# Mish of the last edge group and the last node chunk: from a rational form on VectorE to Exp, Ln and Tanh on ScalarE

## The chip, the cores and the metric

The kernel runs on one core of one Trainium2 chip. A core has five engines that run side by side, each with its own instruction queue in a fixed order: TensorE (PE in the profile; its weight loads are PEld), VectorE (DVE), ScalarE (ACT), GpSimd (POOL) and SyncE (SP). The metric is the time of one execution in microseconds (us). The median of three runs before the change is 1883.51 us (1879.14 to 1885.42).

## The reference

A network of four layers over a graph of 625 nodes with 512 features and 20000 edges. Each layer normalizes the nodes' features, applies a ReLU, computes messages along the edges, sums them by target node, and adds the result to the features. The change touches only the last of the four layers:

```python
def mish(x):
    return x * jnp.tanh(jax.nn.softplus(x))

# N = 625 nodes, E = 20000 edges (sorted by dst), 512 features, 64 edge features
edge_feat = jnp.concatenate([x[src], x[dst], edge_attr], axis=-1)
h = mish(edge_feat @ W1 + b1)
messages = mish(h @ W2 + b2)
agg = jax.ops.segment_sum(messages, dst, num_segments=x.shape[0])
u = mish(jnp.concatenate([x, agg], axis=-1) @ W3 + b3)
out = u @ W4 + b4
y = x + out
mu = jnp.mean(y, axis=-1, keepdims=True)
var = jnp.mean(jnp.square(y - mu), axis=-1, keepdims=True)
return (y - mu) * jax.lax.rsqrt(var + LN_EPS) * gamma + beta
```

Mish of v is v times tanh(ln(1 + exp(v))). With e = exp(v) and n = (2 + e) * e the factor tanh(ln(1 + e)) is also n / (n + 2), which needs an exponential and a reciprocal only.

## The kernel before

**Tiles and stages.** The 20000 edges are 160 tiles of 125 edges, taken in groups of G = 4, so there are NG = 40 groups, numbered 0 to 39. The 625 nodes are NC = 5 chunks of 125, numbered 0 to 4. All arithmetic is fp32.

`layer3_near` (from L1116) is the last layer. Its loop over steps s (L1349) is a pipeline written out by hand: in step s the first product of group s is computed (`first`), the second product of group s - 2 (`second`, L1235), and the messages of group s - 4 are summed into their target nodes (`sent`, L1251) and, one step later, added to the table `aT` of sums (`collected`, L1274). Instructions wrapped in `keep` stay in program order on their engine, so each engine's order is the order of these calls.

**Mish in the steady state.** A result is first bounded from above on VectorE (`bounded`, L1180, into a tile `uz`, `um` or `uu`), then `quotients` (L1188) puts Exp on ScalarE, then Ln with a bias of 1, then Tanh, for all tiles that are ready in that step; a product on VectorE ends it. ScalarE computes functions from a loaded set of tables; where the next function isn't in the set, a load of another set (ACT_TABLE_LOAD) stands ahead of it. Exp and Tanh stand in one set here, Ln in another, so each round has two loads.

**The last group.** Group 39 is treated apart. `second` bounds its messages `mess` in two halves of two tiles each (L1246 to L1248), 125x1024 elements, into two `uz` tiles. In the step of its second product (L1383 to L1388) ScalarE computes Exp of both halves, then Ln and Tanh of half 0 alone. In `sent` (L1255 to L1258) VectorE makes half 1's mish by the rational form, `times_quotient` (L1197), and then half 0's by one product. After that TensorE sums the group's messages by a product with the one-hot matrix `oh` (L1267, tile `agg`); VectorE copies that out (L1271, `ag`), TensorE transposes it (L1277, `trs`) and VectorE adds it to `aT` (L1278).

**The last chunk.** When the last sums are in `aT`, `update_u(4)` (L1285) multiplies them with the lower half of W3 (L1288, tile `u`), adds the part of the nodes' own features (L1291), and bounds the result (L1183, tile `uu`). ScalarE computes Exp (L1408), and then chunk 3's square root for its normalization (`update_root(3)`, L1328, with a load of its set). VectorE makes the chunk's mish by `times_quotient`. Then come the transposes (`update_turn`, L1302, copied out at L1304), chunk 3's end (`update_end(3)`, L1330: a reciprocal of the root, two operations, an output DMA), and chunk 4's product with W4 in two halves (`update_out`, L1319, tile `o`), its statistics, root and end.

Of the kernel before, what the change touches and what calls it, by code (L numbers as in the profile page):

```python
# [9 lines left out]
F32 = mybir.dt.float32  # L10
F16 = mybir.dt.float16
I32 = mybir.dt.int32
AF = mybir.ActivationFunctionType
ALU = mybir.AluOpType
# [3 lines left out]
D = 512  # L18
# [3 lines left out]
G = 4  # L22
NG = NT // G
# [120 lines left out]
def gnn_body(ctx: ExitStack, tc: tile.TileContext, a: dict, out: bass.AP, consts, near: bool):  # L144

    nc = tc.nc
# [969 lines left out]
    def layer3_near(wts, wm2, own, h_tabs, uh):  # L1116

        keep = tc.keep_in_program_order
        with tc.tile_pool(name="layer3n", bufs=2) as lp, banks("c", 6):
# [3 lines left out]
            edges, zs, ms, us, acc, nodes = {}, {}, {}, {}, {}, {}  # L1123
            W = 32

            def base_of(g):
                return min(max(math.ceil(g * G * PACE - SLACK), 0), N - W)
# [26 lines left out]
            def rows(g):  # L1154

                rt = lp.tile([128, GE], F32, tag="rt", name="rt", bufs=3)
                ge = slice(g * GE, (g + 1) * GE)
                nc.sync.dma_start(rt[:64, :], a["edge_attr_64"][:, ge])
                if g < NW:

                    base = min(max(math.floor(g * G * PACE) - 24, 0), N - 64)
                    keep(nc.sync.dma_start(wx[g][:64, :], a["L3_gnn_W1"][2 * D:, :]))
                    keep(nc.sync.dma_start(wx[g][64:, :], xd[base:base + 64, :]))
                    keep(nc.sync.dma_start(dn[g], bcast(a["dst_row"][0, ge], GE, 64)))
                    keep(nc.vector.tensor_scalar(rt[64:, :], dn[g], float(base), row[64:, :],
                                                 op0=ALU.subtract, op1=ALU.is_equal))
                else:
                    nc.sync.dma_start(rt[64:, :], a["edge_attr_64"][:, ge])
                gs = []
                for j in range(G):  # L1170
                    gs.append(lp.tile([P, D], F32, tag="gath", name="g_s", bufs=12))
                    keep(gather(xs, src_i, g * G + j, gs[-1]))
                edges[g] = rt, gs

            def rows_added(g):

                for j in range(G):
                    keep(gather(xd, dst_i, g * G + j, edges[g][1][j], compute_op=ALU.add))

            def bounded(v, parts, cols, tag, bufs):  # L1180

                u = lp.tile([128, width.get(tag, cols)], F32, tag=tag, name=tag, bufs=bufs)[:parts, :cols]
                keep(nc.vector.tensor_scalar_min(u, v, 20.0))  # L1183
                return u
# [3 lines left out]
            def quotients(v):  # L1188

                for u in v:  # L1190
                    keep(nc.scalar.activation(u, u, AF.Exp))  # L1191
                for u in v:
                    keep(nc.scalar.activation(u, u, AF.Ln, bias=1.0))
                for u in v:
                    keep(nc.scalar.activation(u, u, AF.Tanh))

            def times_quotient(v, e):  # L1197

                n = lp.tile([128, G * D], F32, tag="um", name="n", bufs=1)[:v.shape[0], :v.shape[1]]
                keep(nc.vector.scalar_tensor_tensor(n, e, 2.0, e, op0=ALU.add, op1=ALU.mult))  # L1200
                keep(nc.vector.tensor_scalar_add(e, n, 2.0))
                keep(nc.vector.reciprocal(e, e))
                keep(nc.vector.tensor_mul(n, n, v))
                keep(nc.vector.tensor_mul(v, n, e))

            def flat(v):
                return v.rearrange("p a b -> p (a b)")
# [43 lines left out]
            def sent(g):  # L1251


                m = ms.pop(g)
                if g == NG - 1:  # L1255
                    v = [flat(m[:, 2 * n:2 * n + 2, :]) for n in range(2)]
                    times_quotient(v[1], us.pop(("m", g, 1)))
                    keep(nc.vector.tensor_mul(v[0], v[0], us.pop(("m", g, 0))))  # L1258
                base = base_of(g)
                acc[g] = pools["acc"].tile([128, 128], F32, tag="acc", name="agg3", bufs=2)  # L1260
                o = work.tile([P, G, W], F32, tag="oh", name="oh")
                nc.vector.tensor_tensor(o, iota_f[:, None, base:base + W].to_broadcast([P, G, W]),
                                        dst_f[:, g * G:(g + 1) * G, None].to_broadcast([P, G, W]),
                                        op=ALU.is_equal)
                for j in range(G):
                    for i in range(KD):
                        nc.tensor.matmul(acc[g][i * W:(i + 1) * W, :], o[:, j, :],  # L1267
                                         m[:, j, i * 128:(i + 1) * 128], start=j == 0, stop=j == G - 1,
                                         skip_group_check=True, tile_position=(0, i * W))
                v = lp.tile([128, 128], F32, tag="ag", name="ag", bufs=2)  # L1270
                keep(nc.vector.tensor_copy(v, acc[g]))  # L1271
                acc[g] = v
# [22 lines left out]
            def update_mul(c):  # L1295
                keep(nc.vector.tensor_mul(nodes[c], nodes[c], us.pop(("u", c))))
# [52 lines left out]
            for s in range(NG + 5):  # L1349
                if s + 2 < NG:  # L1350
                    rows(s + 2)
                if NW <= s + 1 < NG:
                    rows_added(s + 1)
                if 6 <= s < 9:
                    later_weights(s - 6)
                if s < NG:
                    first(s)
                if s == 0:
                    for n in range(2):
                        quotients([us["z", 0, n]])  # L1360
                        z = flat(zs[0][:, n])
                        keep(nc.vector.tensor_mul(z, z, us.pop(("z", 0, n))))  # L1362
                if s - 4 in ms and s - 4 < NG - 1:
                    m = flat(ms[s - 4])
                    keep(nc.vector.tensor_mul(m, m, us.pop(("m", s - 4))))
                if s - 3 in ms and s - 3 < NG - 1:
                    us["m", s - 3] = bounded(flat(ms[s - 3]), P, G * D, "um", 1)
                quotients([us[k] for k in (("z", s, 0), ("m", s - 3), *(("u", c) for c in range(NC - 1) if s - 6 == last_of[c])) if k in us])
                for c in range(NC - 2):
                    if s - 9 == last_of[c]:  # L1370
                        update_root(c)
                if s - 1 in zs and s > 1:
                    z = flat(zs[s - 1][:, 0])
                    keep(nc.vector.tensor_mul(z, z, us.pop(("z", s - 1, 0))))
                for c in range(NC - 1):
                    if s - 7 == last_of[c]:
                        update_mul(c)
                if s == 1:
                    second(0)
                    keep(nc.vector.memset(mT, 0.0))  # L1380
                if 1 <= s - 2 < NG:
                    second(s - 2)
                if s - 2 == NG - 1:  # L1383

                    for n in range(2):
                        keep(nc.scalar.activation(us["m", NG - 1, n], us["m", NG - 1, n], AF.Exp))
                    for fn, b in ((AF.Ln, 1.0), (AF.Tanh, 0.0)):
                        keep(nc.scalar.activation(us["m", NG - 1, 0], us["m", NG - 1, 0], fn, bias=b))  # L1388
                for c in range(NC - 1):
                    if s - 7 == last_of[c]:  # L1390
                        update_turn(c)
                    if s - 8 == last_of[c]:
                        update_out(c)
                    if s - 9 == last_of[c] and c < NC - 2:
                        update_end(c)
                if 9 <= s < 9 + NC:
                    biases(s - 9)
                if 0 <= s - 4 < NG:
                    sent(s - 4)
                if 0 <= s - 5:  # L1400
                    collected(s - 5)
                for c in range(NC - 1):
                    if s - 5 == last_of[c]:
                        update_u(c)
            c = NC - 1
            update_u(c)
            e = us.pop(("u", c))
            keep(nc.scalar.activation(e, e, AF.Exp))  # L1408
            update_root(c - 1)
            times_quotient(nodes[c], e)  # L1410
            update_turn(c)
            update_end(c - 1)
            update_out(c)
# [19 lines left out]
    with tc.tile_pool(name="wts3", bufs=1) as wts:  # L1433
# [3 lines left out]
        if near:  # L1437
            keep = tc.keep_in_program_order
# [67 lines left out]
```

## Time and profile before

| | |
|---|---|
| median of 3 runs | 1883.51 us (1879.14 to 1885.42) |
| profiled execution | 1883.0 us |
| its span | 1881.2 us |
| mean granted TensorE clock | 0.983 |
| TensorE busy | 1772.1 us, 94% of the span |
| VectorE busy | 1074.1 us, 57% |
| ScalarE busy | 741.3 us, 39% |
| GpSimd busy | 809.9 us, 43% |
| chain that ended last | TensorE 83%, VectorE 11%, ScalarE 2%, DMA 2%, issue 1% |

The profile is of one execution, recorded by the chip's hardware profiler. Times in its rows count from the span's start. A group of equal operations is shown as line, engine, operation, output tile and inputs, shapes (partitions x elements) and count; `<-` in brackets names what ended the wait before it. "The chain that ended last" is followed back from the last instruction, at each step to what released it. Busy shares are averages over the whole span; a change in the last 50 us is read from those 50 us. The granted clock is what the throttle gave TensorE, as a part of full speed.

### The profile page before, as it was taken

How to read it: one execution, taken by the hardware profiler on the slowest of the kernel's cores; microseconds unless marked ns; L12 is line 12 of the kernel's file. 1: busy time of each engine (PE TensorE's matmuls, PEld its weight loads, DVE VectorE, ACT ScalarE, POOL GpSimd, SP SyncE). 2: the span in 40 equal slices, each digit the busy share in tenths (PEclk: the TensorE clock that was granted, in tenths of full speed). 3: DMA queues.
4: the chain of work that ended last, by engine and by line, in shares of the span. 5: the costliest groups of instructions: out<-in, count | busy, mean ns of one | idle time of the engine just before them, and what ended most of it. 6: DMA issues, size and time to landing. Idle time of an engine off the chain costs nothing.

```text
span 1881.2 us, 25801 instructions
## 1 busy us (share of the span) xinstructions
PE 1772.1 (94%) x10688; PEld 960.7 (51%) x10688; DVE 1074.1 (57%) x1877; ACT 741.3 (39%) x856; POOL 809.9 (43%) x478
## 2 busy tenths in 40 slices
PE   5999999999999999999999989999999999999993
PEld 5999844444444444445455444444454444545441
DVE  8999611001100267768774657786676676666655
ACT  1122211000000312222221766767776777668670
POOL 0000000000000077556543688888887888788200
PEclk9999999999999989999999989999999999999996
DMA  2000103003000176565443589666675666666200
GB/s 70 2 2 2 52 0 140 0 0 93 2 0 0 30 187 162 139 146 161 125 119 98 116 150 172 127 122 119 109 132 114 115 132 116 109 119 125 36 0 13
DMA packets 157223, 162.68 MB, mean 86 GB/s; under 512 B 97546, under 2 KB 104059, under 8 KB 157096
## 3 DMA queue, kind: packets, MB, share of 16 engines
q0 software_dynamic: 131584, 119.48, 32.4%
q1 hardware_dynamic: 20100, 32.69, 5.7%
q10 hardware_dynamic: 5412, 8.77, 1.7%
q8 instruction: 86, 1.41, 0.3%
q14 instruction: 41, 0.34, 0.1%
HBM read 155.11 MB, written 5.12 MB: 85 GB/s over the span
## 4 chain that ended last, share of the span: by engine, by line
PE 83%; DVE 11%; ACT 2%; DMA 2%; issue 1%; POOL 0%; DVEq 0%; SPq 0%; ACTq 0%; POOLq 0%
PE z L1243 29%; PE agg L557 9%; PE hb L544 7%; PE sum L856 7%; PE tpw L834 5%; DVE rh L441 4%; PE z L1224 4%; PE z L1229 4%; DVE ohs L450 2%; PE agg L1267 2%; PE xsd L932 2%; PE mlp L786 2%; PE agg L533 2%; PE l L509 2%; PE nsum L502 1%
## 5 line engine op out<-in xcount | busy, mean ns | idle before, releaser
L1243 PE MATMUL z<-wm,z 128*125 128x512 f32 x1280 | 556.9, 593 | 2.7 <-DVE z L1362 2.7
L1243 PEld LDWEIGHTS z<-wm,z 128*125 128x125 f32 x1280 | 237.5, 188 | 293.5 <-issue 268.8
L230 POOL DMA_INDIRECT g_s<-xs,src_i x160 | 303.4, 1896 | 126.1 <-issue 75.5
L230 POOL DMA_INDIRECT g_s<-xd,dst_i x144 | 300.6, 2087 | 43.9 <-issue 42.0
L798 POOL MEMSET mT<- 128x5000 f32 x1 | 4.3, 4267 | 633.4 <-PE agg L557 633.4
L230 POOL DMA_INDIRECT gup<-up,src_i x160 | 198.1, 1238 | 132.0 <-DVE msg L841 60.6
L455 PE MATMUL q<-rh,ohs 125*128 125x160 bf16 (+1 forms) x2400 | 184.5, 238 | 13.5 <-ACT cnt L467 11.0
L455 PEld LDWEIGHTS <-ohs 125*128 125x128 bf16 x2400 | 180.0, 99 | 17.8 <-issue 15.0
L1245 DVE TENSOR_TENSOR mess<-z,b 125x512 f32<-125x512 f32 x160 | 106.4, 687 | 136.4 <-PE z L1243 136.4
L557 PE MATMUL agg<-hb,adj 125*125 125x512 f32 x400 | 173.6, 592 | 0.0
L547 DVE COPY hb<-hb 125x512 f32<-125x512 f32 x20 | 13.8, 692 | 261.0 <-PE hb L544 261.0
L856 PE MATMUL sum<-msg,ohy 125*32 125x128 f32 (+1 forms) x2560 | 146.0, 303 | 8.5 <-issue 6.9
L841 DVE TENSOR_TENSOR msg<-tpw,gup 125x768 f32<-125x768 f32 x160 | 152.0, 950 | 0.0
L856 PEld LDWEIGHTS sum<-msg,ohy 125*32 125x32 f32 x2560 | 101.2, 109 | 86.7 <-issue 85.7
L1231 DVE TENSOR_SCALAR z<-z,b 128x500 f32<-128x500 f32 (+1 forms) x164 | 108.4, 719 | 59.4 <-PE z L1229 57.5
L544 PE MATMUL hb<-basis,hT 128*125 128x512 f32 x320 | 138.6, 592 | 0.0
L1191 ACT ACTIVATE uz<-uz 128x2000 f32<-128x2000 f32 (+1 forms) x41 | 75.0, 1830 | 153.0 <-DVE uz L1183 153.0
L557 PEld LDWEIGHTS agg<-hb,adj 125*125 125x125 f32 x400 | 74.8, 188 | 94.7 <-issue 94.7
L549 ACT COPY hb<-hb 125x512 f32<-125x512 f32 x20 | 11.7, 586 | 258.3 <-PE hb L544 238.4
L839 DVE TENSOR_TENSOR msg<-tpw,gup 125x256 f32<-125x256 f32 x160 | 67.0, 419 | 62.9 <-PE tpw L834 31.1
L1191 ACT ACTIVATE um<-um 125x2048 f32<-125x2048 f32 x39 | 74.6, 1912 | 71.1 <-DVE um L1183 71.1
L544 PEld LDWEIGHTS hb<-basis,hT 128*125 128x125 f32 x320 | 60.1, 188 | 77.3 <-issue 76.8
(187 smaller groups left out, 2240.5 us busy)
## 6 DMA issues: line engine op xcount, KB each, us to landing
rt<-in_edge_attr SPq DMA_DIRECT2D x76, 125.0 KB
basis<-in_L_gnn_basis SPq DMA_DIRECT2D x8, 1024.0 KB
gup<-up,src_i POOLq DMA_INDIRECT x160
g_s<-xs,src_i POOLq DMA_INDIRECT x160
g_s<-xd,dst_i POOLq DMA_INDIRECT x144
w<-in_L_gnn_W SPq DMA_DIRECT2D x2, 1024.0 KB
loop<-in_L_gnn_loop SPq DMA_DIRECT2D x2, 1024.0 KB
w1ab<-in_L_gnn_W ACTq DMA_DIRECT2D x1, 2048.0 KB
```

The costliest lines, as they stand in the source:

```text
L230: return nc.gpsimd.indirect_dma_start(out=dst, out_offset=None, in_=table, in_offset=bass.IndirectOffsetOnAxis(ap=idx[:, t:t + 1], axis=0) ...
L441: keep(nc.vector.tensor_mul(rh, eq[:, :, None, :].to_broadcast([P, G, 3 * NQ + 1, W]), parts[:, t0:t0 + G, :, None] .to_broadcast([P, G, 3 ...
L455: nc.tensor.matmul(q[c][:, :n, o:o + W], os_[:, c, :], rh[:, j, q0:q0 + n, :], start=i + j + k == 0, stop=i == 1 and j == G - 1 and k == 2 ...
L544: nc.tensor.matmul(p[:P, :], hT[:, k, s * P:(s + 1) * P], basis[b][:, k, :], start=k == 0, stop=k == KD - 1)
L557: nc.tensor.matmul(acc[c], adj[:, s - 1, l * NB + b, c * P:(c + 1) * P], hb[:, b, :], start=False, stop=s == NC and b == NB - 1)
L834: nc.tensor.matmul(p[:P, :], hid[s // 2][s % 2][rws, i * P:(i + 1) * P], w4[rws].rearrange("p k u -> p (k u)"), start=True, stop=True)
L841: nc.vector.tensor_mul(m[:, :, 1:, :], pv[:, 2:4, None, :].to_broadcast([P, 2, 3, MUL]), g[:, None, 1:, :].to_broadcast([P, 2, 3, MUL]))
L856: nc.tensor.matmul(A[r * W:(r + 1) * W, c * MUL:c * MUL + v.shape[1]], oh[:, j, q, :], v, start=j % G == 0 and r not in done, stop=j % G = ...
L1191: keep(nc.scalar.activation(u, u, AF.Exp))
L1231: keep(nc.vector.tensor_scalar(zv[:, n, f, :], pf[f][:, :ne], b1[:, f:f + 1], None, op0=ALU.add))
L1243: nc.tensor.matmul(p[:P, :], z[:, j // w, f, j % w * P:(j % w + 1) * P], wm2[:, f, :], start=f == 0, stop=f == KD - 1)
L1245: keep(nc.vector.tensor_add(m[:, j, :], p[:P, :], bc["b2"]))
```

## The change

The last group's two halves both go through Exp, Ln and Tanh on ScalarE. Ahead of them stands an explicit load of a set that holds Exp and Ln together (`set_of_exp`), so that Exp and Ln of one half follow each other without a load; Tanh of both halves comes after one more load, and then the set with Exp and Ln is loaded again. In `sent`, VectorE multiplies half 0 and then half 1 by their factors. The last chunk's mish is made by `quotients` and one product (`update_mul`), with chunk 3's square root after it in ScalarE's queue. `times_quotient` and its scratch tile `n` are gone.

```diff
-            def times_quotient(v, e):
-
-                n = lp.tile([128, G * D], F32, tag="um", name="n", bufs=1)[:v.shape[0], :v.shape[1]]
-                keep(nc.vector.scalar_tensor_tensor(n, e, 2.0, e, op0=ALU.add, op1=ALU.mult))
-                keep(nc.vector.tensor_scalar_add(e, n, 2.0))
-                keep(nc.vector.reciprocal(e, e))
-                keep(nc.vector.tensor_mul(n, n, v))
-                keep(nc.vector.tensor_mul(v, n, e))
+            def set_of_exp():
+
+                keep(nc.scalar.preload_act_table_set("natural_log_exp_and_others"))
...
                 if g == NG - 1:
-                    v = [flat(m[:, 2 * n:2 * n + 2, :]) for n in range(2)]
-                    times_quotient(v[1], us.pop(("m", g, 1)))
-                    keep(nc.vector.tensor_mul(v[0], v[0], us.pop(("m", g, 0))))
+                    for n in range(2):
+                        v = flat(m[:, 2 * n:2 * n + 2, :])
+                        keep(nc.vector.tensor_mul(v, v, us.pop(("m", g, n))))
...
                 if s - 2 == NG - 1:
-
-                    for n in range(2):
-                        keep(nc.scalar.activation(us["m", NG - 1, n], us["m", NG - 1, n], AF.Exp))
-                    for fn, b in ((AF.Ln, 1.0), (AF.Tanh, 0.0)):
-                        keep(nc.scalar.activation(us["m", NG - 1, 0], us["m", NG - 1, 0], fn, bias=b))
+                    v = [us["m", NG - 1, n] for n in range(2)]
+                    set_of_exp()
+                    for u in v:
+                        keep(nc.scalar.activation(u, u, AF.Exp))
+                        keep(nc.scalar.activation(u, u, AF.Ln, bias=1.0))
+                    for u in v:
+                        keep(nc.scalar.activation(u, u, AF.Tanh))
+                    set_of_exp()
...
             update_u(c)
-            e = us.pop(("u", c))
-            keep(nc.scalar.activation(e, e, AF.Exp))
+            quotients([us["u", c]])
             update_root(c - 1)
-            times_quotient(nodes[c], e)
+            update_mul(c)
             update_turn(c)
             update_end(c - 1)
```

## The prediction

> **What bounds the kernel now.** I read the page's span first, then the chain that ended last in its closing stretch, because the edit touches only the last group of edges and the last chunk of nodes; then ScalarE's timeline there; then the granted clock.
>
> ```profile
> span 1881.2 us, 25801 instructions
> ```
>
> The chain after the last dense TensorE work (in order of time: start, duration, what):
>
> ```profile
> 1828.94 0.70 DVE mess L1245
> ...
> 1835.53 1.15 DVE n L1200
> ...
> 1836.70 0.70 DVE uz L1201
> ...
> 1837.43 6.55 DVE uz L1202
> 1843.98 1.09 DVE n L1203
> ...
> 1846.32 1.15 DVE mess L1258
> ...
> 1847.60 1.97 PE agg L1267 x32
> ...
> 1850.80 6.57 PE u L1288 x8
> ...
> 1858.64 0.64 ACT uu L1408
> ...
> 1860.49 3.35 DVE uu L1202
> ...
> 1865.17 1.11 PE tr L1302 x4
> ```
>
> Until 1828.92 the chain is TensorE's second products; from there it is serial and short of overlap. VectorE owns 1835.53 to 1847.46, over half of it the 6.55 us reciprocal over 125x1024, and again about 5.9 us at 1859.30, 3.35 of it the reciprocal over 125x512. TensorE is idle for both.
>
> ScalarE's timeline over the same stretch (start, duration, engine, line, operation, tile; in brackets the idle time before and its releaser):
>
> ```profile
> 1825.90 1.91 ACT L1195 ACTIVATE um<-um 125x2048 f32<-125x2048 f32 x1
> 1827.71 1.04 ACT L1386 ACTIVATE uz<-uz 125x1024 f32<-125x1024 f32 x1
> 1830.40 1.06 ACT L1386 ACTIVATE uz<-uz 125x1024 f32<-125x1024 f32 x1 [1.64 <-DVE uz L1183]
> 1831.47 1.28 ACT L1388 ACT_TABLE_LOAD   x1
> 1832.77 1.06 ACT L1388 ACTIVATE uz<-uz 125x1024 f32<-125x1024 f32 x1
> 1833.84 1.28 ACT L1388 ACT_TABLE_LOAD   x1
> 1835.14 1.06 ACT L1388 ACTIVATE uz<-uz 125x1024 f32<-125x1024 f32 x1
> 1858.64 0.63 ACT L1408 ACTIVATE uu<-uu 125x512 f32<-125x512 f32 x1 [22.45 <-DVE uu L1183]
> 1859.29 1.28 ACT L1328 ACT_TABLE_LOAD   x1
> ```
>
> A function over 125x1024 is 1.05 us, over 125x512 0.63, a load 1.28, and the gap after each of them 0.01 to 0.03. ScalarE then sits 22.45 us idle beside VectorE's long work.
>
> **The change, part by part.** The last group's second half and the last chunk leave the rational form on VectorE (five operations with a reciprocal) for Exp, Ln, Tanh on ScalarE and one VectorE product. Other stages keep their instructions and their order on every engine.
>
> Part 1, the last group. ScalarE is busy with group 38's Tanh until 1825.90 + 1.91 = 1827.81. Then, in the new queue order, each step with 0.02 between:
> - load of a set that holds Exp and Ln together: 1827.83 to 1829.11. New. It has nothing to hide behind: half 0's bound is ready at 1823.5.
> - Exp half 0: 1829.13 to 1830.18; Ln half 0: 1830.20 to 1831.25.
> - Exp half 1 (bound ready at 1830.36, so no wait; independent of the step before, so 0.09 of overlap, as 1825.90 + 1.91 against 1827.71 shows): 1831.16 to 1832.21; Ln half 1: 1832.23 to 1833.29.
> - load for Tanh: 1833.31 to 1834.59; Tanh half 0: to 1835.67; Tanh half 1: 1835.58 to 1836.64.
> - load back to Exp with Ln: to 1837.94. It is covered: the next ScalarE work is the last chunk's Exp, due about 1848, so some 10 us of VectorE and TensorE work hide it; without cover it would cost 1.28.
>
> The last Tanh ends 0.44 later than before (1836.20), though six functions and two loads now stand after group 38's Tanh where four and two did: before, ScalarE waited 1.64 for half 1's bound in between.
>
> VectorE: queued ahead of the products are group 38's product (1830.68, 2.28), its copy and group 37's add, done at 1835.53 as before. The product of half 0 waits for its Tanh: 1835.70 to 1836.92 (1.22, the row of L1258). That of half 1 follows: 1836.84 to 1838.06. Behind these two waiting products on VectorE are only this group's copy out and its adds; TensorE waits for them. TensorE's sixteen agg products now wait in two places: eight need half 0 alone. The first eight (half of 1.97, 0.99) start 0.14 after the product, as before: 1837.06 to 1838.05; the others 1838.20 to 1839.19. Before, agg ended at 1849.57. **Part 1: -10.4 us.** Bounds: all sixteen agg products waiting for half 1 would give 1840.2, -9.4; -10.6 is the other end, with Ln overlapping the dependent Exp.
>
> Where the stall goes: with reciprocal and quotient gone, ScalarE's Tanh (1835.67) and VectorE's own queue (1835.53) come out even, so ScalarE is now the late one, by 0.15 us for half 0.
>
> Part 2, the last chunk. From the copy of agg to the bound (1849.57 to 1858.6) nothing changes but its place. Before, Exp's start to the transposes: 1865.17 - 1858.64 = 6.53. After: Exp 0.63, Ln 0.63, load 1.28, Tanh 0.63, product about 0.65 (0.63 by L1203's row, 0.69 by L1291's), four gaps of 0.02 and 0.04 to TensorE: 3.94. The load before Exp is the covered one of part 1. **Part 2: -2.6 us** (ends -2.4 and -2.8).
>
> Chunk 3's square root moves behind the last Tanh in ScalarE's queue; load and root end 0.02 + 1.28 + 0.02 + 0.29 = 1.6 after it. Its VectorE reader stands behind the copy of the transposes, which ends 0.02 + 0.65 + 0.04 + 1.11 + 0.02 + 0.69 = 2.5 after that Tanh. So its cost is nothing, with 0.9 in hand; the cover is the product, the transposes and the copy. If it were late, chunk 3's output and then the adds of chunk 4 wait behind it on VectorE. The final root finds its set loaded, as before. No DMA is added; the output's issues on SP and ScalarE keep their place relative to the last stage.
>
> Sum: -10.4 - 2.6 = -13.0. The profiled execution took 1883.0 (span 1881.2 and 1.8 around it), giving 1870.0; the median of the runs shown is 0.5 higher, giving **1870.5**.
>
> **Two rules of the Trainium skill against rows.** First, loads. In the trace all loads of this last layer take 1.28 with the next function 0.01 to 0.02 later. The skill ("ScalarE: Activation LUTs", section "What ACT_TABLE_LOAD costs") adds a drain of about 1.38 to each switch. Three loads are now on the path (first, for Tanh, for the last chunk's Tanh): by the rule the gain falls to 13.0 - 4.1 = 8.9 and the time is 1874.6. I take the row, where no such gap appears.
>
> Second, the clock. Granted clock by stretch (the first value after the busy times):
>
> ```profile
> 1831.00:1833.00 2.00, 0.00 (x0) 0.00 (x0) 2.00 (x2) 1.97 (x3) 0.00 (x0) 0.92 0.00 0
> 1856.00:1857.40 1.40, 1.35 (x3) 0.33 (x1) 0.01 (x1) 0.00 (x0) 0.00 (x0) 0.79 0.00 0
> 1857.40:1862.00 4.60, 0.00 (x0) 0.00 (x0) 3.74 (x5) 2.21 (x3) 0.00 (x0) 0.78 0.00 0
> 1870.00:1871.00 1.00, 1.00 (x5) 0.82 (x5) 0.37 (x1) 0.00 (x0) 0.00 (x0) 0.88 0.30 86
> ```
>
> The clock is 1.00 or 0.50, so 0.92 over 2 us puts the fall at 1832.68; likewise a rise at 1856.59, a fall at 1859.98 and a rise at 1870.24. The distances are 23.9, 3.4 and 10.3: 7, 1 and 3 times 3.41. So the u products (6.57) and the o products (5.28) run mostly at half clock, and how much depends on where a 3.41 us grid falls. The skill ("TensorE: Matmul & The Clock Gate", Part 1) says the same: a window of 3.4 us that runs free of the kernel. By the row, u and o stay at 11.85 together. By the rule they move: after the change the u products start 16.24 - 2.59 = 13.65 before the o products, which is four windows, so both see the same phase. Each would last about 6.97 fully cold, less half of what remains after the first full window: together 10.0 to 13.4, mean 11.7. I take the row; the rule gives -1.9 to +1.5 for the range. It speaks against a hope that shorter idle keeps TensorE warm: the gaps that remain (about 5 us before the transposes, and the 2 us before agg, already at 0.50 in the trace) are long enough for the fall.
>
> **The rivals.**
> - Loads drain (above): 1874.6. For it the rule; against it every load row.
> - ScalarE's chain is longer than its rows, so the gain shrinks to within the measurement. Three Ln wait for an Exp just ahead of them on the same engine, and the trace has no such pair without a load between; VectorE's dependent pairs have 0.03. At 0.3 each that is +0.7 to 0.9, 1871.4; to lose all but 5.6 us it would take over 2 us each. Little speaks for that; time then about 1878 to 1883.
> - Slower: the set with Exp and Ln together is not among those this run has loaded before (by the set numbers in the built program Ln came from one set until here, Exp and Tanh from another), and its first load, at 1827.83, stands on the path. If it had to be fetched from memory at that moment, everything waits. It decides from 13.0 us over the usual 1.28, and shows as slower from 18.7 us over; I put that at 1892. Against it: every load of every set so far, first ones included, shows 1.28, and the skill's same section says that all sets are put into the engine's backing slots at the start, with one price for every set. Part 1's other loads repeat a set already used.
> - The change does nothing, as when the order moved by itself: excluded by the built instruction order, in which VectorE loses eight operations (ten of the rational form against two products more) and ScalarE gains four functions and two loads, at the places used above.
>
> **How the numbers follow.** A difference below 0.3% (5.65 us) about cannot be told from no change here; the runs shown spread over 6.3. Forecast as worked out 0.85 at 1870.5, with its own range 1867 to 1874 (clock phase -1.9 to +1.5, part 1 -0.2 to +1.0, part 2 0.2, and about 2 for the median of a few runs). Drained loads 0.08 at 1874.6. Chain longer 0.04, at 1878 to 1883. First load fetched 0.03, at 1892. The range over the cases: 1866 to 1875.5, which takes in the drained loads and leaves out the last two (0.07) and the far ends of the first. Faster: 0.85 + 0.08 = 0.93; same 0.04; slower 0.03.
>
> **What would show each step.** ScalarE: load at about 1827.8, then four functions with no load between, the last Tanh of 125x1024 ending near 1836.6. VectorE: no reciprocal wider than one column in the tail, the two products near 1835.7 and 1836.8. TensorE: agg in two runs of half the count, ending near 1839.2; u starting near 1840.4; transposes about 5.2 after u's end rather than 7.8. Wrong would be: a load longer than 1.28, a gap of over 0.1 at a dependent Ln, agg in one piece after half 1, chunk 3's root releasing VectorE after the copy, or u and o together outside 10.0 to 13.4.

## The result and the profile after

The changed kernel takes 1874.99 us (median of 20 runs, 1868.45 to 1879.90); the kernel before, run again beside it, takes 1887.32 (20 runs, 1879.14 to 1898.46). The ratio is 0.9938, with a 95% interval of 0.9928 to 0.9949: 11.7 us faster (9.6 to 13.6); the two medians differ by 12.3. The forecast was a gain of 13.0 and a time of 1870.5. The profiled execution took 1874.9.

```profile
span 1873.0 us, 25799 instructions
```

The chain that ended last in the profile after, from group 38's last Tanh on (start, duration, what); it answers to the chain shown of before:

```profile
1829.79 1.91 ACT um L1195
...
1831.72 1.28 ACT L1199
...
1833.01 1.07 ACT uz L1382
...
1834.10 1.06 ACT uz L1383
1835.16 0.96 ACT uz L1382
...
1836.14 1.06 ACT uz L1383
...
1837.21 1.28 ACT L1385
...
1838.51 1.07 ACT uz L1385
...
1839.60 1.24 DVE mess L1253
...
1840.97 2.19 PE agg L1262 x32
...
1844.39 6.41 PE u L1283 x8
...
1852.07 0.64 ACT uu L1191
...
1854.67 0.64 ACT uu L1195
...
1856.08 1.11 PE tr L1297 x4
...
1857.94 6.46 PE o L1314 x16
```

The reciprocals are gone; ScalarE's functions carry the chain from group 38's Tanh to the first product. Each of ScalarE's steps starts 0.01 to 0.03 after the one before, the dependent Ln (1834.10 after 1833.01 + 1.07) among them.

These times can't be held against the first profile directly, because the last dense product (the 32 matmuls of group 39's `second`) starts at 1818.91 here and at 1815.01 before. From here on the text counts from that start; the stretch from it to the end of the span is called the tail. In TensorE's timeline of before and of after:

```profile
1815.01 13.90 PE L1243 MATMUL z<-wm,z 128*125 128x512 f32 x32
...
1833.02 1.93 PE L1267 MATMUL agg<-mess,oh 125*32 125x128 f32 x32 [2.06 <-DVE mess L1365]
...
1847.60 1.94 PE L1267 MATMUL agg<-mess,oh 125*32 125x128 f32 x32 [11.74 <-DVE mess L1258]
...
1850.80 6.56 PE L1288 MATMUL u<-wm3b,aT 128*125 128x512 f32 x8 [0.38 <-DVE aT L1278]
...
1865.17 1.09 PE L1302 MATMUL tr<-ident,u 125*128 125x125 f32 x4 [7.82 <-DVE u L1204]
1867.04 5.28 PE L1319 MATMUL o<-wm,uT 128*125 128x256 f32 x16 [0.77 <-DVE uT L1304]
```

```profile
1818.91 13.90 PE L1238 MATMUL z<-wm,z 128*125 128x512 f32 x32
...
1840.97 2.12 PE L1262 MATMUL agg<-mess,oh 125*32 125x128 f32 x32 [1.21 <-DVE mess L1253]
...
1844.39 6.39 PE L1283 MATMUL u<-wm3b,aT 128*125 128x512 f32 x8 [0.38 <-DVE aT L1273]
...
1856.08 1.09 PE L1297 MATMUL tr<-ident,u 125*128 125x125 f32 x4 [5.29 <-DVE u L1291]
1857.94 6.45 PE L1314 MATMUL o<-wm,uT 128*125 128x256 f32 x16 [0.77 <-DVE uT L1299]
```

The agg at 1833.02 is group 38's, the last of each view group 39's. That one ends 34.53 after the start before (1847.60 + 1.94 - 1815.01), and 24.18 after it now: 10.35 earlier. From the last chunk's Exp to the transposes it is 6.53 before and 4.01 now: 2.52 less. The two make 12.87. But u and o together take 11.84 before and 12.84 now, so the tail falls by 12.10 only, from 66.19 to 54.09. And the 3.9 us by which the tail starts later would hide a third of the gain if they belonged to the change. So three questions went to experiments: do the two parts carry what the sum says; what do the loads and the split cost; and what is behind u, o and the late start.

### The profile page after: what moved, and what is told of

Its sections match the earlier page's. It is cut to its first block, busy times and chain, and to the rows that moved or that the text cites. A ratio compares the mean times of both kernels' runs of the same rounds, so it can differ in the third digit from the quotient of the medians.

```text
span 1873.0 us, 25799 instructions
## 1 busy us (share of the span) xinstructions
PE 1779.9 (95%) x10688; PEld 964.2 (51%) x10688; DVE 1060.8 (57%) x1869; ACT 747.1 (40%) x862; POOL 809.5 (43%) x478
## 4 chain that ended last, share of the span: by engine, by line
PE 82%; DVE 11%; ACT 3%; DMA 2%; issue 1%; POOL 1%; DVEq 0%; SPq 0%; POOLq 0%; ACTq 0%
PE z L1238 28%; PE agg L557 9%; PE hb L544 7%; PE sum L856 7%; PE tpw L834 5%; DVE rh L441 4%; PE z L1224 4%; PE z L1219 4%; DVE ohs L450 2%; PE mlp L786 2%; PE agg L1262 2%; PE agg L533 2%; PE l L509 2%; PE xsd L932 2%; PE nsum L502 1%
## 5 line engine op out<-in xcount | busy, mean ns | idle before, releaser
L230 POOL DMA_INDIRECT g_s<-xs,src_i x160 | 296.3, 1852 | 126.0 <-issue 75.8
L230 POOL DMA_INDIRECT g_s<-xd,dst_i x144 | 307.7, 2137 | 43.9 <-issue 43.0
L547 DVE COPY hb<-hb 125x512 f32<-125x512 f32 x20 | 13.8, 692 | 262.6 <-PE hb L544 262.6
L549 ACT COPY hb<-hb 125x512 f32<-125x512 f32 x20 | 11.7, 586 | 259.8 <-PE hb L544 239.8
```

The costliest lines, as they stand in the source:

```text
L230: return nc.gpsimd.indirect_dma_start(out=dst, out_offset=None, in_=table, in_offset=bass.IndirectOffsetOnAxis(ap=idx[:, t:t + 1], axis=0) ...
```

## Experiments

Spans and times differ between the sets of runs (before takes 1887.3, 1854.1, 1853.9 and 1882.5 us in the four of them), so each ratio is against the kernel before in the same set, on the same chip. The table has all profiles, in us; "agg ends after" is counted from the start of the tail to the end of group 39's agg, and "rest" is the tail without u and o.

| profile | tail starts at | agg ends after | u | o | tail | rest |
|---|---|---|---|---|---|---|
| before | 1815.01 | 34.53 | 6.56 | 5.28 | 66.19 | 54.35 |
| `b_again` (before) | 1791.77 | 34.53 | 6.64 | 5.32 | 66.13 | 54.17 |
| after | 1818.91 | 24.18 | 6.39 | 6.45 | 54.09 | 41.25 |
| `a_again` (after) | 1790.10 | 24.17 | 5.65 | 6.07 | 53.40 | 41.68 |
| `a_timed` (after) | 1813.11 | 24.18 | 6.22 | 6.36 | 53.89 | 41.31 |
| `p1_group` | 1783.13 | 24.19 | 5.28 | 6.34 | 55.37 | 43.75 |
| `p2_chunk` | 1793.46 | 33.67 | 6.05 | 6.28 | 63.14 | 50.81 |
| `l4_loads` | 1783.90 | 29.32 | 6.16 | 6.33 | 58.90 | 46.41 |
| `a_auto` | 1779.36 | 26.73 | 5.96 | 5.59 | 56.74 | 45.19 |
| `o_swap` | 1783.10 | 26.08 | 6.29 | 6.39 | 55.90 | 43.22 |
| `w_warm` | 1785.71 | 23.75 | 3.70 | 3.72 | 47.69 | 40.27 |
| `w_again` | 1814.06 | 23.75 | 3.70 | 3.72 | 47.74 | 40.32 |
| `w_late` | 1817.49 | 24.18 | 6.09 | 3.72 | 50.71 | 40.90 |

### Each part alone

`p1_group` keeps the rational form for the last chunk:

```diff
-            quotients([us["u", c]])
+            e = us.pop(("u", c))
+            keep(nc.scalar.activation(e, e, AF.Exp))
             update_root(c - 1)
-            update_mul(c)
+            times_quotient(nodes[c], e)
```

> Part 1 alone: the last group goes to ScalarE as in the change, the last chunk keeps its rational form on VectorE. 'Tail' is the stretch from the first second product of group 39 on TensorE to the end of the span: 66.2 us before, 54.1 after the change in their profiles. Theory (costs add along the chain, the rest is the phase of the clock): agg of group 39 ends 10.4 us earlier than before against that start, nothing else moves, so the tail is 55.8 with u and o at 11.85 together (54.0 to 57.3 over the phases), and the time is 10.4 us or 0.55% below before (ratio 0.9945). Rival (the two parts overlap or the gain of part 1 is eaten elsewhere): the tail stays above 58 us, ratio 0.997 or more.

Measured: ratio 0.9946 (0.9930 to 0.9961), tail 55.37, agg 10.34 earlier. As the theory has it; the rival falls.

`p2_chunk` is the kernel before with the last chunk's edit, and the load for it behind the last group's Tanh:

```diff
-            e = us.pop(("u", c))
-            keep(nc.scalar.activation(e, e, AF.Exp))
+            quotients([us["u", c]])
             update_root(c - 1)
-            times_quotient(nodes[c], e)
+            update_mul(c)
```

> Part 2 alone: the last group keeps the form of before, the last chunk goes to ScalarE, with the load of the set for Exp and Ln behind the last group's Tanh. Theory: Exp's start to the transposes takes 3.95 us in place of 6.5; tail 63.6 (61.9 to 65.3 over the clock's phases), time 2.6 us or 0.14% below before (ratio 0.9986). Rival (chunk 3's square root, moved behind Tanh, comes too late for VectorE): its reader waits for ScalarE after the copy of the transposes and the gain is below 1.5 us.

Measured: ratio 0.9985 (0.9975 to 0.9996), tail 63.14. VectorE and ScalarE in its timeline:

```profile
1838.34 0.63 ACT L1195 ACTIVATE uu<-uu 125x512 f32<-125x512 f32 x1
1838.98 1.28 ACT L1328 ACT_TABLE_LOAD   x1
1839.00 0.69 DVE L1296 TENSOR_TENSOR u<-u,uu 125x512 f32<-125x512 f32 x1 [3.36 <-ACT uu L1195]
...
1840.28 0.29 ACT L1328 ACTIVATE rstd<-mv,eps 125x1 f32<-125x1 f32 x1
1840.88 0.68 DVE L1304 COPY uT<-tr 128x500 f32<-128x500 f32 x1 [1.19 <-PE tr L1302]
1841.47 0.15 DVE L1332 RECIPROCAL rstd<-rstd 125x1 f32<-125x1 f32 x1
```

Chunk 3's root is done at 1840.57 and its reader on VectorE starts at 1841.47, without a wait, so the rival falls: 0.9 in hand, as forecast. In this profile the tail fell 0.5 more than expected. TensorE's timeline of it:

```profile
1811.47 1.08 PE L1267 MATMUL agg<-mess,oh 125*32 125x128 f32 x32 [2.06 <-DVE mess L1365]
...
1825.20 1.93 PE L1267 MATMUL agg<-mess,oh 125*32 125x128 f32 x32 [11.73 <-DVE mess L1258]
```

Group 38's agg ran at full clock in it (1.08 us against 1.93 in the first profile), and VectorE's rational form stands behind that group's copy: agg of group 39 ends 0.86 earlier (33.67 against 34.53). u and o were 0.5 longer. In the changed kernel the first of these can't show: agg of group 39 ends 24.17 to 24.18 after the start, whether agg of group 38 took 1.93 (after) or 1.08 (`a_again`, `a_timed`), because ScalarE sets the end there.

### The price of a load

`l4_loads` puts four more loads of sets ahead of the last group's first Exp:

```diff
                     v = [us["m", NG - 1, n] for n in range(2)]
+                    for _ in range(2):
+                        set_of_exp()
+                        keep(nc.scalar.preload_act_table_set("exp_and_others"))
                     set_of_exp()
```

> The changed kernel with four more loads of sets ahead of the first Exp of the last group, where ScalarE sets the end. Row theory: a load costs 1.28 and 0.02, so the last group is 5.2 us later; tail 59.3 (57.5 to 60.8 over the clock's phases), ratio to before about 0.9966. Rule theory (each switch also drains, 2.66 in all): 10.6 us later, tail 64.8, ratio about 0.9994.

ScalarE's timeline of this run:

```profile
1796.70 1.28 ACT L1199 ACT_TABLE_LOAD   x1
1797.99 1.28 ACT L1382 ACT_TABLE_LOAD   x1
1799.28 1.28 ACT L1199 ACT_TABLE_LOAD   x1
1800.57 1.28 ACT L1382 ACT_TABLE_LOAD   x1
1801.86 1.28 ACT L1199 ACT_TABLE_LOAD   x1
1803.15 1.06 ACT L1385 ACTIVATE uz<-uz 125x1024 f32<-125x1024 f32 x1
```

agg ends 5.14 later than in the changed kernel (29.32 against 24.18), 1.285 for each load; ratio 0.9962 (0.9947 to 0.9977). The row theory holds. The 1.38 of drain that the Trainium skill ("ScalarE: Activation LUTs", section "What ACT_TABLE_LOAD costs") adds to a switch doesn't show here. The first load of the set with Exp and Ln costs the same 1.28 (1831.72 in the profile after), so the rival of a fetched set falls too.

`a_auto` leaves the explicit loads out, and the builder places them by its own rule:

```diff
                     v = [us["m", NG - 1, n] for n in range(2)]
-                    set_of_exp()
...
                         keep(nc.scalar.activation(u, u, AF.Tanh))
-                    set_of_exp()
```

> The changed kernel without the two explicit loads; the builder then puts a load ahead of each function that is not in the set in place, with Exp and Tanh in one set and Ln in another. Theory by rows: four loads instead of two stand between group 38's Tanh and the last Tanh, 2.6 us later, and one more stands between Exp and Ln of the last chunk, 1.3; tail 58.0 (56.2 to 59.6 over the clock's phases), 3.9 us above the changed kernel, ratio to before about 0.9959. Rival (loads are hidden behind waits for VectorE's bounds): tail 54 to 55, ratio 0.994.

Measured: agg 2.55 later than in the changed kernel, and 5.29 from the last chunk's Exp to the transposes (1814.64 to 1819.93) against 4.01, 1.28 more; together 3.8, as expected. The rest is 45.19 against 41.25 to 41.68. By time alone it would not be seen: the ratio is 0.9942 (0.9927 to 0.9958), which takes in the rival's 0.994 and just leaves out the theory's 0.9959; it is the rows of the profile that decide. In this profile u and o were 1.3 us shorter than in the one on which the expected ratio rested.

### The order of the halves

```diff
-                    for n in range(2):
+                    for n in (1, 0):
                         v = flat(m[:, 2 * n:2 * n + 2, :])
```

> The changed kernel with VectorE's two products of the last group in the other order (half 1, then half 0), so that TensorE's first sums wait for both. Theory: product of half 1 waits for the last Tanh, half 0 follows, and all of agg after it: 1.85 us later; tail 55.9, ratio to before about 0.9948. Rival (the split does nothing, TensorE was waiting for both in any case): no difference from the changed kernel.

Measured: agg ends 1.90 later and runs in one piece; the rest is 43.22. Order and split together are worth what was expected, and the rival falls. The ratio, 0.993 (0.991 to 0.995), is too wide to tell it from the changed kernel.

### Same kernels, profiled again

`b_again` and `a_again` are the two kernels without an edit.

> The kernel before, profiled once more. Theory: the tail is 66.2 again within the clock's phases (64.5 to 67.8), and the start of the last second product, 1815.0 in the first profile, moves by some us with the time that the clock is at one half where TensorE has short pauses, above all at the start of the third layer (about 645 to 680 us). Rival: the start stays at 1815 within 1 us, so that the 3.9 us by which it came later in the changed kernel's profile belong to the change.

> The changed kernel, profiled once more. Theory: the tail is 54.1 again within the clock's phases (52.2 to 55.7); the start of the last second product, 1818.9 in the first profile, moves as that of the kernel before. Rival: it stays at 1819 within 1 us.

On this chip the tail starts at 1791.8 in the kernel before and 1790.1 in the changed one. It starts between 1779.4 and 1791.8 in the four profiles of this chip (these two, `a_auto`, `o_swap`), and between 1783.1 and 1793.5 in the four of the chip of `p1_group`; up to that point the code is the same. So a difference of 3.9 us is well inside what the same code does from one execution to the next, and nothing ties it to the change. Of the first pair of profiles it can be seen where it arose. The stretch of 640 to 680 us, in which the third layer starts, of before and then of after (length, busy times, then the granted clock):

```profile
640.00:680.00 40.00, 35.88 (x219) 15.55 (x218) 18.10 (x41) 14.15 (x27) 21.68 (x16) 0.87 0.42 111
```

```profile
640.00:680.00 40.00, 37.19 (x196) 16.08 (x197) 15.60 (x36) 13.78 (x24) 20.25 (x14) 0.70 0.38 103
```

At 0.87 the clock was at one half for 10.4 us (0.13 x 2 x 40), at 0.70 for 24.0. The third layer's first `tpw` product starts at 660.1 and at 663.7: nearly all of the 3.9. Over all profiles this is not the only source: the third layer itself, from its first `tpw` product to its last, takes 298 to 309 us in these eight profiles and 325 to 334 in the other five, and what sets that was not tried.

`a_timed` is the changed kernel once more, timed on another chip.

> The changed kernel once more, now timed. Theory: chain sum of the two parts, 12.8 to 13.0 us below before, ratio about 0.9932; its tail less u and o is 41.3 as in its two profiles before, and u and o together 11.7 to 12.9. Rival (the change loses a little elsewhere): ratio 0.9945 or more with the same tail.

Ratio 0.9931 (0.9906 to 0.9956), tail 53.89, rest 41.31. The theory's number, but the interval takes in the rival's.

### TensorE's clock in the tail

`w_warm` gives TensorE matmuls to do where it is idle in the tail. Their result is read by nobody:

```diff
+            def warm(n):
+
+                p = ps("warm")
+                for _ in range(n):
+                    keep(nc.tensor.matmul(p[:, :128], ident, wm2[:, 0, :128], start=True, stop=True))
...
+                if g >= NG - 2:
+                    warm(7 if g == NG - 2 else 13)
                 for j in range(G):
                     for i in range(KD):
                         nc.tensor.matmul(acc[g][i * W:(i + 1) * W, :], o[:, j, :],
...
             update_mul(c)
+            warm(22)
             update_turn(c)
```

> The changed kernel with matmuls whose result nobody reads in TensorE's idle gaps of the tail: 20 around the sums of groups 38, 22 between u and the transposes. Clock theory: the granted clock stays at 1.00, u and o take about 3.5 us each in place of 6.4 and 6.45, agg of 39 about 0.5 less, transposes 0.5 less; tail about 47 us, 7 below the changed kernel's profile and about 6 below its mean; ratio to before about 0.9905. Rival (u and o are slow for another reason, such as waiting for operands after a pause): the fillers change nothing or delay what follows them, tail 54 or more, ratio 0.9938 or more.

TensorE's timeline from group 39's agg on:

```profile
1807.77 0.64 PE L1270 MATMUL agg<-mess,oh 125*32 125x128 f32 x16 [1.00 <-DVE mess L1259]
...
1808.81 0.65 PE L1270 MATMUL agg<-mess,oh 125*32 125x128 f32 x16 [0.40 <-DVE mess L1259]
...
1810.58 3.70 PE L1291 MATMUL u<-wm3b,aT 128*125 128x512 f32 x8 [0.38 <-DVE aT L1281]
1814.11 5.08 PE L1205 MATMUL warm<-wm,ident 128*128 128x128 f32 x44
...
1819.66 0.62 PE L1305 MATMUL tr<-ident,u 125*128 125x125 f32 x4 [0.47 <-DVE u L1299]
...
1821.05 3.72 PE L1322 MATMUL o<-wm,uT 128*125 128x256 f32 x16 [0.77 <-DVE uT L1307]
```

u, transposes and o take 3.70, 0.62 and 3.72 in place of 6.39, 1.09 and 6.45. The granted clock is 1.00 in every stretch from 1800 to 1825. Tail 47.69, ratio 0.9895 (0.9879 to 0.9912). The rival falls: u and o, with the same operands, were slow by their clock.

> The changed kernel with all fillers on TensorE, as before. Theory: tail 47.7 again with little spread, since no phase of the clock is left in it; time 5 to 7 us below the changed kernel on the same chip, ratio to before about 0.990.

Ratio 0.9903 (0.9877 to 0.9929), tail 47.74, 0.05 from the first; 1862.54 us against 1869.25 of the changed kernel on the same chip. This version beats both kernels.

`w_late` keeps the 22 fillers between u and the transposes alone.

> The changed kernel with the 22 fillers between u and the transposes alone. Clock theory: u starts at half clock as without fillers (5.3 to 6.6); the clock rises in the first full window of about 3.4 us inside u or just after it and the fillers keep it, so transposes take 0.6 and o 3.7: tail about 50.9 (49.5 to 52). If the rise comes late, the fillers themselves run at half clock for some us and delay the transposes by up to 1 us. Rival (o is slow because of its operands): o stays at 6 and more, tail 54.

u 6.09, o 3.72, transposes 0.62, tail 50.71, ratio 0.9904 (0.9873 to 0.9935). About half of the gain is had with one line, after u; the clock had risen before the fillers began, and they ran in 5.07.

## Why the prediction was right and wrong

The mechanism came out as it was written: which engine ends each step, which loads are hidden, and both parts to 0.1 us from the first profile of before to that of after. What failed is the size of three terms: the base from which 13.0 was taken (3.8 us, the largest), and two that were read off a single row while TensorE's clock sets them, u and o at 11.85 and group 38's sums ahead of VectorE's queue.

**Part 1** (-10.4) measured -10.34 to -10.36 in three profiles of the changed kernel and in `p1_group`. ScalarE's chain came out step by step: load, Exp, Ln, Exp, Ln with 0.02 between, load, Tanh. TensorE's sums start 0.14 after the first product (1840.83 to 1840.97 in the chain), as the split says. The row joins their two runs into one of 2.12, against 1.94 for one piece in `o_swap`; in `w_warm` they stand apart, 16 each. What the split is worth alone (1.0 by the sum) wasn't measured, since `o_swap` (1.90) also puts the product that waits for the later Tanh first.

The step of part 1 that held by luck is "done at 1835.53 as before". In the row group 38's sums run at half clock (1.93), and before the change VectorE's rational form waits for them. With these sums at full clock agg of group 39 ends at 33.67 before (`p2_chunk`) and still at 24.18 after, and part 1 is 9.5. In the eleven profiles without fillers ahead of them, these sums took 1.08 or 1.09 in six, 1.47 and 1.56 in two, 1.93 or 1.94 in three, both of before among the last. Their mean is 1.39, which makes part 1 about 9.8 over many executions (an estimate: 10.35 less 0.86 x 0.54 / 0.85).

**Part 2** (-2.6) measured -2.52; the product takes 0.69 and not 0.65, and the last gap is a little longer. Chunk 3's root cost nothing, with the 0.9 in hand that was named.

**The loads** cost their row, not the page's price. Those of `l4_loads` follow one another; in `a_auto`, with functions between them, two more made agg 2.55 later, 1.275 each. The rivals of drained loads, of a longer chain and of a set fetched at first use are all excluded.

**The clock** was the term taken as the row, 11.85 for u and o on both sides. The three profiles of the changed kernel have 12.84, 11.72 and 12.58, mean 12.4; the two of before 11.84 and 11.96, mean 11.9. So 0.5 of the gain goes there in these five profiles. It was inside the range given for it, but neither the row nor the rule's mean of 11.7 met it. The working's own sizes were short: 6.97, less half of what remains after the rise, gives 6.38 for u and 5.09 for o on the rows that it was read from, which have 6.57 and 5.28. With 0.2 more for each, the rule has 10.4 to 13.8, mean 12.1 (an estimate). In both profiles of before a late rise of the clock in u goes with an early one in o (6.56 with 5.28; 6.64 with 5.32). The working had found that the changed spacing of 13.65 is four windows, so that u and o would go together, and they do (6.39 with 6.45, 5.65 with 6.07, 6.22 with 6.36); but it then kept the old sum as the middle value. The spacing holds u itself, so it is 13.55, 12.81 and 13.38 in the three, and four windows only nearly. Stretches of the profile after (granted clock after the busy times):

```profile
1836.00:1837.00 1.00, 0.09 (x4) 0.09 (x8) 1.00 (x2) 0.97 (x2) 0.00 (x0) 0.60 0.00 0
1849.00:1850.00 1.00, 1.00 (x3) 0.43 (x2) 0.00 (x0) 0.00 (x0) 0.00 (x0) 0.57 0.00 0
...
1853.00:1855.00 2.00, 0.00 (x0) 0.00 (x0) 0.00 (x0) 1.97 (x3) 0.00 (x0) 0.57 0.00 0
...
1863.00:1864.00 1.00, 1.00 (x4) 0.83 (x4) 0.00 (x0) 0.00 (x0) 0.00 (x0) 0.75 0.00 0
```

With the clock at 1.00 or 0.50 these put a fall at 1836.2, a rise at 1849.86, a fall at 1853.28 and a rise at 1863.5: 13.7, 3.4 and 10.2 apart, or 4, 1 and 3 windows, as the Trainium skill ("TensorE: Matmul & The Clock Gate", Part 1) describes them. The rise in u comes 5.5 after its start, and that in o 5.6.

The rise in u, in this order in `a_again`, `a_timed` and `p1_group` (the same chain up to u):

```profile
1819.00:1820.00 1.00, 1.00 (x3) 0.52 (x2) 0.00 (x0) 0.00 (x0) 0.00 (x0) 0.73 0.00 0
```

```profile
1843.00:1844.00 1.00, 1.00 (x3) 0.52 (x2) 0.00 (x0) 0.00 (x0) 0.00 (x0) 0.65 0.00 0
```

```profile
1811.00:1812.00 1.00, 1.00 (x2) 0.33 (x1) 0.00 (x0) 0.00 (x0) 0.00 (x0) 0.59 0.00 0
```

It comes 4.0, 5.1 and 3.2 after u's start, and u took 5.65, 6.22 and 5.28: 3.7, its length at full clock in `w_warm`, and half of that time, to 0.05. That of after (5.5, u 6.39) and that of before (1856.59, so 5.8, u 6.56) fit the same sum. Counted from the start of the tail, in windows of 3.41, the rises leave 2.2, 3.3 and 1.4 here, 0.3 in after and 0.7 in before; over all thirteen profiles, whose code is the same up to there, the window's edge lies between 0.2 and 3.3. So its phase isn't tied to the kernel. That the two profiles of before met nearly the same phase (0.7 and 0.8) is chance, and nothing shows that the 0.5 belongs to the change.

**The base** is the step that failed for the absolute time. Three runs gave 1883.51 as the median before; 20 runs, with these three and the lowest of all among them, give 1887.32, which is 3.8 higher. Less 13.0 that is 1874.3, and 1875.0 was measured. The text called 0.3% about what can be told from no change, and set only "about 2" for the median of a few runs into the likeliest case's range, though the three runs spread over 6.3. The likeliest case's own range of 1867 to 1874 was missed. That 1875.0 lies inside the whole range is luck: its upper end of 1875.5 was there for the drained loads. Their 1874.6 is the closest of all the forecast's numbers, and yet it isn't what happened, as `l4_loads` shows; their gain of 8.9 also lies outside 9.6 to 13.6.

By ratio, -11.7 (9.6 to 13.6) agrees with -12.9 for the chain. Group 38's sums at full clock in part of the executions would take about 0.5 from that, and u and o 0.5 more if their difference were real; which of it is there, the intervals can't tell.

Left open: how often group 38's sums run at half clock in the timed runs, and what sets the third layer's length.

## What to carry to other kernels

In a serial tail a change's worth can be added up from the rows of one profile to 0.2 us, if the engine that will be last is found for each step and TensorE's clock is the same in the rows compared: one group of sums at half or full clock made 0.9 us here. The total time of a run, which varies by several us in code that the edit doesn't touch, is the wrong place to look for a part of 2 us, and a stretch counted from a common instruction is the right one. Where TensorE waits several us for other engines, its next products start at half clock: price them so, and try cheap matmuls in the gap, ahead of the work that has to be fast. A base taken from three runs needs its own uncertainty in the range.

## What was not expected of the hardware

The clock is worth as much as half of the whole change: 20 + 22 small fillers, which use TensorE's idle time, brought 6.7 us (1869.25 to 1862.54; 6.2 in the tails). It didn't take full occupation to keep the clock up: with fillers TensorE was busy 82% of 1800 to 1810, with waits of up to 1.0 us, and the clock stayed at 1.00. To raise it took more. Windows on the 3.41 us grid that the falls and rises fit, one of before, one of `b_again` and one of after (length, then busy times, TensorE first, then the granted clock):

```profile
1866.81:1870.23 3.42, 3.19 (x8) 2.55 (x9) 1.64 (x4) 0.00 (x0) 0.00 (x0) 0.50 0.12 30
```

```profile
1826.68:1830.09 3.41, 3.00 (x4) 1.33 (x5) 0.46 (x2) 0.00 (x0) 0.00 (x0) 0.50 0.00 0
```

```profile
1832.79:1836.20 3.41, 1.61 (x35) 1.03 (x34) 3.32 (x5) 3.34 (x5) 0.00 (x0) 1.00 0.00 0
```

At half clock 93% busy raised it (the clock is 1.00 from 1870.24 on), and 88% didn't. At full clock 47% dropped it at 1836.2, when TensorE had been idle for only 1.35 us, since 1834.85. The windows of all thirteen profiles, from 25 us ahead of the tail to the end, fit this: none with 88% or less raised the clock and all with 93% or more did; none with more than 47% dropped it and all with less than 43% did. So less work keeps the clock than raises it. The shares are those of TensorE's rows; that the chip counts the same was not shown.
